# Reordering ScalarE's and GpSimd's work inside one loop of a two-layer convolution kernel

## The chip, the cores and the metric

The kernel runs on one core of one Trainium2 chip. The metric is the device time of one execution in microseconds (us), lower is better. Time before: 3071.7 us, the median of three runs (3067.76 to 3073.29).

## The reference, cut to what matters

The input x is 4 images of 64 channels and 256 x 256 points, all in fp32. Two residual layers follow each other. The change touches the first layer only:

```python
def _L0_conv_ref(x, ...):            # called with _gn(x): group norm, 32 groups
    h = _gelu(_conv2d(x, c1_w, ((1, 1), (1, 1))) + c1_b)       # 3x3, 64 -> 64
    h = _c1x1(h, c2_w, c2_b)                                   # 64 -> 128
    xa, k = jnp.split(h, 2, axis=1)
    xs = _conv2d(xa, sh_w, ((0, 0), (1, 1)), groups=C) + sh_b  # 1x3 per channel
    xs = _conv2d(xs, sv_w, ((1, 1), (0, 0)), groups=C) + sv_b  # 3x1 per channel
    xs = _gelu(xs)
    ...                              # gate from the mean of xs, keeps 2 of 3 experts
    for i, (w1, b1, w2, b2, w3, b3) in enumerate(experts):
        e = _c1x1(_c1x1(k, w2, b2) * _c1x1(xs, w1, b1), w3, b3)
        out = out + e * mask[:, i]
    return _c1x1(out, proj_w, proj_b)
x = x + _L0_conv_ref(_gn(x), ...)
x = x + _L1_conv_ref(_gn(x), ...)    # 3x3, batch norm, relu, 3x3, batch norm, relu
```

## The kernel before, in words

**Units and slots.** Layer 0 is cut into 64 units of 16 image rows (16 units to an image; 128 partitions are two row blocks of 64 channels). One loop runs over 67 slots; in slot u the 3x3 convolution of unit u is made, while unit u+1 is prepared and units u-1 and u-2 go through the taps that follow. A slot has no barrier at its end: each engine has its own list of instructions, executes it in order, and waits by semaphores for the others.

**The order is written by hand.** `at_slot(u, pos, call, ...)` files a call under slot u and a position. Positions 0 to 6 make the first half of a slot and 6 to 12 the second. All calls are sorted by slot and position, and every engine's list is exactly in that order. The position decides therefore only what stands ahead of what on one engine.

**What a slot does**, with the lines of the profile:

- The 3x3 convolution is of Winograd's kind along rows. GpSimd makes six combinations of rows of x, called `v`. TensorE multiplies them in three products: `front_conv(u, (1, 2))`, `(3, 4)` and `(0, 5)` (matmuls `ps_c<-v,us` of L492; `ps_c` has two PSUM buffers). ScalarE copies two results out (`front_copy`, `mc`, L594), VectorE combines them in four steps (`butterfly_a` to `butterfly_d`, L599 to L618), and ScalarE ends with Gelu (`front_h`, `h`, L626).
- To make `v` for unit u+1: ScalarE multiplies rows of x by 4 (`x_four`, `x4`, L526) and later others by 2 and by 4 (`x_scaled`, `e` and `x`, L540 and L542). GpSimd makes two differences with `x4` (L532), four differences of x in place (L535; both in `x_differences`), then `v` 1 to 4 (`v_inner`, L556 to L559) and `v` 0 and 5 (`v_outer`, L563 and L564).
- The taps: for each half unit TensorE makes `front_taps_a` and `front_taps_b` (`ps_a<-h,av`, L492) into the one PSUM buffer `ps_a`. Between the two stands `divide`: GpSimd writes one word (`tick`, L485) after the last matmul of taps_a, and the first matmul of taps_b waits for it. ScalarE then makes `t` (`front_taps_i`, L666), VectorE adds two shifted copies (`front_taps_h`, L672, L675, L678), after which `ps_a` is free; ScalarE's second Gelu gives `xs` (`front_xs`, L694).
- In even slots TensorE makes `ps_k`, which ScalarE copies out (L716); in odd slots it makes `ps_q`, which VectorE takes (L729). Both use the one PSUM buffer `ps_p`.
- **Statistics** of the next image's x, for its group norm: `stats_piece` (L432), on ScalarE. A piece is two instructions of 128 x 1024 points with a sum each (an Identity with a shift, then a Square in place, each followed by a read of the accumulator). Image 1's pieces fall into slots 1 to 11, some three to a slot; image 2's into slots 12 to 27 and image 3's into slots 28 to 43, two to a slot.
- **The output of layer 0** (`plan_out`: loads, `ps_o` matmuls, VectorE's `y`, L831 and L836, stores) of an earlier image runs beside the loop from slot 19 on. All DMAs are issued from SyncE's queue.

So the loop has four stages: slots 1 to 11 (three pieces a slot), 12 to 18 (two pieces), 19 to 43 (two pieces and an output), 44 to 62 (an output, no pieces). Layer 1 follows.

Of the kernel before, what the change touches and what calls it, by code (L numbers as in the profile page):

```python
# [13 lines left out]
ALU = mybir.AluOpType  # L14
# [14 lines left out]
NOCT = NG // 2  # L29
CG = 4  # L30
CPAIR = CG * GP
NCH = NG // CG
# [9 lines left out]
def conv_preact_kernel(ctx: ExitStack, tc: tile.TileContext, io, col128, colset, col64):  # L42
    nc = tc.nc
# [466 lines left out]
    def x_edges(u):  # L510

        b, k = divmod(u, NCH)
        for at_k, half, row in ((0, 0, 0), (NCH - 1, 1, 9)):
            if k == at_k and u > 0:
                rows = slice(half * C, half * C + C)
                edge = xt[u][rows, row, :]
                nc.gpsimd.tensor_scalar(edge, zeros[rows, 0:W], gn1[b][rows, 0:1], None, ALU.add)

    def x_rows(u, j):
        return xt[u][:, j : j + 5 : 4, :]  # L520
# [4 lines left out]
        inner = xt[u][:, 1:9, :].rearrange("p (g r) w -> p r g w", r=4)[:, 0:2]  # L525
        nc.scalar.activation(x4s[u], inner, AF.Copy, scale=4.0)  # L526

    def x_differences(u):

        x, x4 = xt[u], x4s[u]  # L530
        for j in (1, 2):
            nc.gpsimd.tensor_tensor(x4[:, j - 1], x_rows(u, j + 2), x4[:, j - 1], ALU.subtract)  # L532
        x_edges(u)
        for r in range(0, 8, 2):
            nc.gpsimd.tensor_tensor(x[:, r : r + 2], x[:, r + 2 : r + 4], x[:, r : r + 2], ALU.subtract)  # L535

    def x_scaled(u):

# [5 lines left out]
    def at_v(i):  # L544
        return v[:, i, :, 1 : 1 + W]

    def v_pads(b):
        edges = zeros[:, 0:4].rearrange("p (a b) -> p a b", b=2)
        nc.gpsimd.tensor_scalar(v[:, 1, :, 0 : PW : PW - 1], edges, gn1[b][:, 0:1], -6.0, ALU.add, ALU.mult)

    def v_inner(u):

        if u % NCH == 0 and u > 0:
            v_pads(u // NCH)
        p, q2, e2 = x4s.pop(u), x_rows(u, 2), e2s.pop(u)
        nc.gpsimd.tensor_tensor(at_v(1), p[:, 1], p[:, 0], ALU.add)  # L556
        nc.gpsimd.tensor_tensor(at_v(2), p[:, 1], p[:, 0], ALU.subtract)
        nc.gpsimd.tensor_tensor(at_v(3), q2, e2, ALU.add)
        nc.gpsimd.tensor_tensor(at_v(4), q2, e2, ALU.subtract)  # L559

    def v_outer(u):

# [138 lines left out]
    def front_k(b, j):  # L701

        ps = bank("p", f"ps_k_{b}_{j}").rearrange("p s a b -> p s (a b)")
        for t in range(2):
            for i in range(4):
                for s in range(2):
                    half = slice(s * C, s * C + C)
                    nc.tensor.matmul(
                        ps[32 * i : 32 * i + 32, s],
                        wk[half, s, t, :],  # L710
                        hs[NCH * b + 2 * j + i // 2][half, t, i % 2 * 2 : i % 2 * 2 + 2, :].rearrange("p a b -> p (a b)"),
                        start=(t == 0),
                        stop=(t == 1),
                    )
        k_sb[b, j] = work.tile([P, 2, GF], F32, tag="k", name=f"k_{b}_{j}", bufs=1)
        nc.scalar.activation(flat(k_sb[b, j]), ps.rearrange("p s f -> p (s f)"), AF.Identity, bias=k_bias)  # L716

# [279 lines left out]
    def at_each(places, chain):  # L997
# [8 lines left out]
    TAIL = {  # L1006
        (0, 1.15): (0, 1.15), (0, 1.55): (0, 1.55), (0, 4.7): (0, 4.7), (0, 2): (0, 2), (0, 2.2): (0, 2.2),
        (0, 4): (0, 13.2), (0, 4.15): (0, 13.3), (0, 5.2): (0, 13.4), (0, 5.3): (0, 13.5), (0, 8.6): (1, 13.9),
        (0, 7): (2, 13.2), (0, 7.2): (2, 13.25), (0, 8): (3, 13.1), (0, 9): (3, 13.2), (0, 9.1): (3, 13.3),
        (1, 1.15): (3, 13.4), (1, 1.55): (3, 13.5), (1, 4.7): (4, 13.9), (1, 2): (5, 13.2), (1, 2.2): (5, 13.25),  # L1010
        (1, 4): (6, 13.2), (1, 4.15): (6, 13.3), (1, 5.2): (6, 13.4), (1, 5.3): (6, 13.5), (1, 8.6): (7, 13.9),
        (1, 8): (8, 13.2), (1, 8.1): (8, 13.3),
# [2 lines left out]
    def at_slot(u, pos, call, *args):  # L1015

        step, order = (2 * u, pos) if pos < 6 else (2 * u + 1, pos - 6)
        if u >= UNITS:
            step, order = TAIL[u - UNITS, pos]
            step += CONV1  # L1020
        at(step, order, call, *args)

    def plan_front():
        last = UNITS - 1
        at_slot(0, 0, x_load, 2)
        at_slot(0, 1.25, next, first_end, None)
        at_slot(0, 1.36, next, first_end, None)
        for u in range(SLOTS):
            if u + 3 <= last:
                at_slot(u, 0, x_load, u + 3)  # L1030
            if u <= last:
                at_slot(u, 1, front_conv, u, (1, 2))
                at_slot(u, 1.1, front_copy, u, 0)
                at_slot(u, 1.3, front_conv, u, (3, 4))
                at_slot(u, 1.35, butterfly_a, u)
                at_slot(u, 1.4, front_copy, u, 1)
                at_slot(u, 2.1, butterfly_b, u)
                at_slot(u, 4.05, butterfly_c, u)
                at_slot(u, 6.12, butterfly_d, u)
                at_slot(u, 6.13, front_h, u, True)  # L1040
                at_slot(u, 5, front_conv, u, (0, 5))
                at_slot(u, 6.14, front_h, u, False)
            if u + 1 <= last:
                at_slot(u, 0.5, x_differences, u + 1)
                at_slot(u, 1.5, x_scaled, u + 1)
                at_slot(u, 2.3, v_inner, u + 1)
                at_slot(u, 5.5, v_outer, u + 1)
            if u + 2 <= last:
                at_slot(u, 4.3, x_four, u + 2)
            if 0 <= u - 2 <= last:  # L1050
                at_slot(u, 2, front_taps_a, u - 2, 1)
                at_slot(u, 2.2, divide)
                at_slot(u, 4, front_taps_b, u - 2, 1)
                at_slot(u, 4.15, front_taps_i, u - 2, 1)
                at_slot(u, 5.2, front_taps_h, u - 2, 1)
                at_slot(u, 5.3, front_xs, u - 2, 1)
                at_slot(u, 8.6, xs_store, u - 2, 1)
            if 0 <= u - 1 <= last:
                at_slot(u, 7, front_taps_a, u - 1, 0)
                at_slot(u, 7.2, divide)  # L1060
                at_slot(u, 9, front_taps_b, u - 1, 0)
                at_slot(u, 9.1, front_taps_i, u - 1, 0)
                at_slot(u + 1, 1.15, front_taps_h, u - 1, 0)
                at_slot(u + 1, 1.55, front_xs, u - 1, 0)
                at_slot(u + 1, 4.7, xs_store, u - 1, 0)
            j = (u - 2) // 2
            if u % 2 == 0 and 0 <= j < UNITS // 2:
                at_slot(u, 8, front_k, *divmod(j, NOCT // 4))
            if u % 2 and 0 <= j < UNITS // 2:
                at_slot(u, 8, front_q, *divmod(j, NOCT // 4))  # L1070
                at_slot(u, 8.1, front_low, *divmod(j, NOCT // 4))
        for b in range(B):
            t = NCH * (b + 1)
            if b < B - 1:
                places = (t + 1, 8.3), (t + 2, 1.25), (t + 2, 1.36), (t + 2, 1.52), (t + 2, 6.15), (t + 2, 8.3), (t + 2, 9.06)
                chain = gate(b)
                for place in places:
                    at_slot(*place, next, chain, None)
            else:
                at_each(((CONV1 + 12 + n, 12.7) for n in (1, 3, 3, 4, 8, 12, 16)), gate(b))  # L1080

        at_slot(1, 1.6, weights1_load)
        at_slot(3, 6.2, weights1_top)
        chain = weights1_scale()
        at_slot(4, 1.45, next, chain, None)
        at_slot(4, 6.2, next, chain, None)
        for i, name in enumerate(("w1", "w2")):
            chain = weights1(name)
            for n in range(3):
                at_slot(7 + 3 * i + n, 6.2, next, chain, None)  # L1090

    def plan_stats(b):

        t = NCH * (b - 1) - (4 if b > 1 else -1)
        per = 11 / NCH if b == 1 else 1
        slots = [t + per * k for k in range(NCH)]
        for k in range(NCH):
            at_slot(max(int(slots[k] - 2), 0), 1.5 if slots[k] >= 3 else 0.1, stats_load, b, k, "s", 4)
            if k == 0:
                at_slot(int(slots[0]), 0.95, stats_shift, b)  # L1100
            for i in range(2):
                s = slots[k] + i * per / 2
                first = s - int(s) < 0.5
                for part in range(2):
                    at_slot(int(s), ((1.12, 4.4) if first else (6.5, 7.15))[part], stats_piece, b, 2 * k + i, part)
        e = NCH * b - 4
        places = (e, 8.3), (e + 1, 1.25), (e + 1, 1.36), (e + 2, 1.25), (e + 2, 1.36), (e + 2, 1.52), (e + 2, 6.15), (e + 3, 1.25), (e + 3, 1.36)
        chain = stats_end(b)
        for place in places:
            at_slot(*place, next, chain, None)  # L1110
        at_slot(NCH * b - 1, 5.15, scale_weights, b)
# [280 lines left out]
    for i, (b, k) in enumerate(steps):  # L1392
# [9 lines left out]
        j = i - 3 + KEEP  # L1402
# [113 lines left out]
```

## Time and profile before

| | |
|---|---|
| median of 3 runs | 3071.7 us |
| the profiled execution | 3069.24 us |
| its span, first to last instruction | 3067.4 us |
| mean granted TensorE clock | 0.911 |
| PE busy / VectorE / ScalarE / GpSimd, share of the span | 77% / 80% / 67% / 55% |
| layer 0's loop in the span | from 63.6 us to about 1340 us |

The shares are means over stages with different limits, and are to be read stage by stage. Start to start, by the first `mc` (L594) of each unit, the slots took:

| slots | us per slot |
|---|---|
| 1 to 5 | 17.4 to 18.4 |
| 6 to 11 | 19.4 to 20.9 |
| 12 to 18 | 17.9 to 22.4, mean 19.5 |
| 19 to 43 | mostly 19.85 and 20.85 in turn; 22 to 24 where a chain of statistics stands between |
| 53 to 61 | 18.93 to 19.00 |

### The profile page before, as it was taken

How to read it: one execution, taken by the hardware profiler on the slowest of the kernel's cores; microseconds unless marked ns; L12 is line 12 of the kernel's file. 1: busy time of each engine (PE TensorE's matmuls, PEld its weight loads, DVE VectorE, ACT ScalarE, POOL GpSimd, SP SyncE). 2: the span in 40 equal slices, each digit the busy share in tenths (PEclk: the TensorE clock that was granted, in tenths of full speed). 3: DMA queues.
4: the chain of work that ended last, by engine and by line, in shares of the span. 5: the costliest groups of instructions: out<-in, count | busy, mean ns of one | idle time of the engine just before them, and what ended most of it. 6: DMA issues, size and time to landing. Idle time of an engine off the chain costs nothing.

```text
span 3067.4 us, 53128 instructions
## 1 busy us (share of the span) xinstructions
PE 2372.5 (77%) x21576; PEld 1519.2 (50%) x21576; DVE 2458.7 (80%) x2793; ACT 2054.9 (67%) x2274; POOL 1675.0 (55%) x1210
## 2 busy tenths in 40 slices
PE   1888889998999999978889999998999999200000
PEld 1444445444444545545566666776888888200000
DVE  5567677888888988867788888988998999886665
ACT  6888877777776655556566767877888888433222
POOL 5877877777677877744345545645555555000000
PEclk9999999999999999999999999998999999655555
DMA  8664579999898989838889988765777764799999
GB/s 339 205 226 188 193 254 338 344 352 327 323 348 297 307 290 315 301 146 294 320 303 343 362 316 326 261 250 195 262 265 260 271 255 142 305 426 427 426 427 405
DMA packets 135573, 915.36 MB, mean 298 GB/s; under 512 B 14944, under 2 KB 15712, under 8 KB 40608
## 3 DMA queue, kind: packets, MB, share of 16 engines
q1 hardware_dynamic: 135328, 911.97, 79.6%
q8 instruction: 169, 2.77, 0.4%
q14 instruction: 76, 0.62, 0.1%
HBM read 573.74 MB, written 338.17 MB: 297 GB/s over the span
## 4 chain that ended last, share of the span: by engine, by line
PE 27%; DMA 18%; DVE 6%; issue 2%; ACT 1%; POOL 1%; SPq 0%; DVEq 0%; ACTq 0%; POOLq 0%
PE ps_h L295 17%; PE ps_h2m L295 6%; DMA y_end<-y_d 5%; DMA h<-h_d 4%; DMA out<-h 3%; DMA y<-in_xp 3%; PE ps_hm L295 3%; DMA xs_in<-xs_d 2%; DVE h L317 1%; PE ps_o L492 1%; DVE diff L352 1%; DVE odd L361 1%; DMA yn<-y_d 1%; DVE y L831 1%; DVE h L1398 1%
## 5 line engine op out<-in xcount | busy, mean ns | idle before, releaser
L295 PE MATMUL ps_h<-diff,w_q 128*128 128x512 f32 x3072 | 754.6, 400 | 11.5 <-DVE h L317 11.5
L295 PEld LDWEIGHTS ps_h<-diff,w_q 128*128 128x128 f32 x3072 | 579.2, 190 | 183.7 <-issue 29.9
L492 PE MATMUL ps_c<-v,us 64*64 64x256 f32 x9216 | 541.2, 383 | 37.4 <-DVE ps_c L612 32.7
L342 POOL TENSOR_TENSOR d<-yn 128x1024 f32<-128x1024 f32 x128 | 355.9, 2801 | 319.1 <-DMA yn<-y_d 182.1
L492 PE MATMUL ps_a<-h,av 64*64 64x512 f32 x4080 | 400.5, 506 | 88.6 <-DVE t L675 69.2
L492 PEld LDWEIGHTS ps_c<-v,us 64*64 64x64 f32 x9216 | 362.9, 135 | 189.0 <-DVE ps_c L612 40.7
L342 POOL TENSOR_TENSOR d<-h 128x1024 f32<-128x1024 f32 x127 | 312.1, 2480 | 194.6 <-DVE diff L350 133.4
L317 DVE SCALAR_TENSOR_TENSOR h<-ps_h,scale_w,m 128x1024 f32<-128x1024 f32 x256 | 323.5, 1279 | 63.5 <-PE ps_h L295 47.3
L492 PEld LDWEIGHTS ps_a<-h,av 64*64 64x64 f32 x4080 | 160.3, 136 | 369.4 <-issue 260.6
L535 POOL TENSOR_TENSOR x<-x 128x512 f32<-128x512 f32 x256 | 328.2, 1282 | 15.5
L672 DVE SCALAR_TENSOR_TENSOR t<-ps_a,m,t 128x1020 f32<-128x1020 f32 x128 | 163.6, 1278 | 201.4 <-ACT t L666 200.7
L1397 ACT ACTIVATE v<-y_end,shift,gn 128x2048 f32<-128x2048 f32 x64 | 133.8, 2092 | 279.2 <-DMA y_end<-y_d 244.0
L381 ACT ACTIVATE junk<-h,less_h 128x2048 bf16<-128x2048 f32 (+3 forms) x133 | 256.0, 1925 | 11.1 <-DVE h L317 10.9
L1398 DVE SCALAR_TENSOR_TENSOR h<-h,ss,v 128x2048 f32<-128x2048 f32 x64 | 149.8, 2350 | 120.2 <-ACT v L1397 120.2
L831 DVE SCALAR_TENSOR_TENSOR y<-ps_o,ob,y 128x1024 f32<-128x1024 f32 x128 | 163.9, 1280 | 90.6 <-PE ps_o L492 43.1
L666 ACT ACTIVATE t<-ps_a,tap_bias,m 128x1024 f32<-128x1024 f32 x128 | 153.8, 1201 | 99.3 <-PE ps_a L492 98.8
L295 PE MATMUL ps_h2m<-odd,w_q 128*128 128x512 f32 x768 | 193.2, 400 | 8.2 <-DVE odd L361 4.4
L694 ACT ACTIVATE xs<-t 128x1024 f32<-128x1024 f32 x128 | 134.5, 1051 | 94.0 <-issue 72.7
L295 PE MATMUL ps_hm<-odd,w_q 128*128 128x512 f32 x768 | 194.2, 402 | 3.7 <-DVE t L675 3.0
L352 DVE SCALAR_TENSOR_TENSOR diff<-d,gn,diff 128x1024 fp32r<-128x1024 f32 x128 | 190.3, 1517 | 4.9 <-ACT diff L345 4.9
L345 ACT ACTIVATE diff<-d 128x1024 fp32r<-128x1024 f32 x128 | 135.1, 1055 | 83.6 <-POOL d L342 82.3
L626 ACT ACTIVATE h<-ps_c,c1b 128x1024 f32<-128x1024 f32 x128 | 135.6, 1110 | 73.3 <-DVE ps_c L618 69.7
(226 smaller groups left out, 4348.0 us busy)
## 6 DMA issues: line engine op xcount, KB each, us to landing
h_d<-h SPq DMA_DIRECT2D x114, 1024.0 KB
x<-in_xc SPq DMA_DIRECT2D x64, 1280.0 KB
h<-h_d SPq DMA_DIRECT2D x64, 1152.0 KB
yn<-y_d SPq DMA_DIRECT2D x60, 1152.0 KB
xs_in<-in_xp SPq DMA_DIRECT2D x64, 1024.0 KB
xs_d<-xs SPq DMA_DIRECT2D x128, 512.0 KB
xs_in<-xs_d SPq DMA_DIRECT2D x64, 1024.0 KB
y<-in_xp SPq DMA_DIRECT2D x64, 1024.0 KB
```

What stands on the lines that cost most here:

```text
L295: nc.tensor.matmul(ps, wq[w][:, kind, kx, :], t[:, rows, kx : kx + W], start=(j == 0), stop=(j == len(terms) - 1))
L317: nc.vector.scalar_tensor_tensor(h.rearrange("p (e k) w -> p e (k w)", e=2), ps.rearrange("p e k w -> p e (k w)"), w_scale[w], m.unsqueeze ...
L342: engine.tensor_tensor(raw.rearrange("p (g r) w -> p g r w", g=2), *pair, ALU.subtract)
L352: nc.vector.scalar_tensor_tensor(lower, raw, scale, upper.bitcast(F32), ALU.mult, ALU.subtract)
L381: nc.scalar.activation(junk[rows, 0:n], flat(h), AF.Square, bias=less[name][rows], accum_out=total)
L492: last[:] = [nc.tensor.matmul(ps[o, at_out[0] : at_out[1], :], w[i], rhs[i], **flags)]
L535: nc.gpsimd.tensor_tensor(x[:, r : r + 2], x[:, r + 2 : r + 4], x[:, r : r + 2], ALU.subtract)
L626: nc.scalar.activation(hs[u][:, :, rows, :], ps, AF.Gelu, bias=c1_bias[u // NCH])
L666: nc.scalar.activation(flat(t), flat(ps), AF.Identity, bias=tap_bias, scale=sh[:, 1:2])
L672: nc.vector.scalar_tensor_tensor(t[:, :, 1:W], ps[:, :, 0 : W - 1], sh[:, 0:1], t[:, :, 1:W], ALU.mult, ALU.add)
L831: nc.vector.scalar_tensor_tensor(y, ps.rearrange("p x s w -> p x (s w)"), out_bias[b], y, ALU.add, ALU.add)
L1398: nc.vector.scalar_tensor_tensor(h, h, ss2[:, 0:1], v, ALU.mult, ALU.add)
```

## The change

The calls are the same, and so is the number of instructions on each engine. On TensorE, VectorE and SyncE the order is the same too; on ScalarE and GpSimd it changes.

- `x_scaled(u+1)` moves from position 1.5 to 1.2: ahead of the second `mc` (1.4).
- `x_four(u+2)` moves from 4.3 to 1.58: ahead of `front_taps_i` (4.15), behind `front_xs` (1.55).
- `x_differences` is cut into three pieces and made a unit sooner: `x_fourths(u+2)` at 2.4, `x_seconds(u+2)` at 6.6 (two instructions) and at 7.3 (two). It was at 0.5 for unit u+1.
- `v_inner(u+1)`: `v` 1 to 3 move from 2.3 to 1.31, ahead of the `tick` at 2.2; `v` 4 stays at 2.3.
- `stats_piece`: in a slot's first half, from 1.12 and 4.4 to 4.35 and 4.4; in the second half, from 6.5 and 7.15 to 5.4 and 9.15. `front_taps_i` of the second half stands at 9.1.
- The copy of `ps_k` moves from 8 to 9.2 (`front_k_out`), behind `front_taps_i`.

```diff
-    def x_differences(u):
-
-        x, x4 = xt[u], x4s[u]
+    def x_fourths(u):
+
+        x4 = x4s[u]
         for j in (1, 2):
             nc.gpsimd.tensor_tensor(x4[:, j - 1], x_rows(u, j + 2), x4[:, j - 1], ALU.subtract)
-        x_edges(u)
-        for r in range(0, 8, 2):
+
+    def x_seconds(u, rows):
+
+        x = xt[u]
+        if 0 in rows:
+            x_edges(u)
+        for r in rows:
             nc.gpsimd.tensor_tensor(x[:, r : r + 2], x[:, r + 2 : r + 4], x[:, r : r + 2], ALU.subtract)
...
-    def v_inner(u):
+    def v_inner(u, part=None):
...
             if u + 1 <= last:
-                at_slot(u, 0.5, x_differences, u + 1)
-                at_slot(u, 1.5, x_scaled, u + 1)
-                at_slot(u, 2.3, v_inner, u + 1)
+                if u == 0:
+                    at_slot(u, 0.5, x_differences, 1)
+                at_slot(u, 1.2, x_scaled, u + 1)
+                at_slot(u, 1.31, v_inner, u + 1, 0)
+                at_slot(u, 2.3, v_inner, u + 1, 1)
                 at_slot(u, 5.5, v_outer, u + 1)
             if u + 2 <= last:
-                at_slot(u, 4.3, x_four, u + 2)
+                at_slot(u, 1.58, x_four, u + 2)
+                at_slot(u, 2.4, x_fourths, u + 2)
+                at_slot(u, 6.6, x_seconds, u + 2, (0, 2))
+                at_slot(u, 7.3, x_seconds, u + 2, (4, 6))
...
             if u % 2 == 0 and 0 <= j < UNITS // 2:
                 at_slot(u, 8, front_k, *divmod(j, NOCT // 4))
+                at_slot(u, 9.2, front_k_out, *divmod(j, NOCT // 4))
...
-                    at_slot(int(s), ((1.12, 4.4) if first else (6.5, 7.15))[part], stats_piece, b, 2 * k + i, part)
+                    at_slot(int(s), ((4.35, 4.4) if first else (5.4, 9.15))[part], stats_piece, b, 2 * k + i, part)
```

## The prediction

> **What bounds the kernel now.** I read the table of slices first: PE is 80 to 99% busy in the loop's part (slices 2 to 17) at nearly full clock, so I ask stage by stage what keeps it from more. The windows by stage (busy time of each engine, then clock, DMA share, GB/s) say how much is missing:
>
> ```profile
> core 0: us, PE busy (x) PEld busy (x) DVE busy (x) ACT busy (x) POOL busy (x), PEclk, DMA share, GB/s
> 80.00:192.00 112.00, 96.83 (x1445) 54.20 (x1439) 65.50 (x85) 100.55 (x149) 99.10 (x91) 0.98 0.65 227
> 192.00:294.00 102.00, 81.61 (x1120) 41.20 (x1116) 69.50 (x87) 84.12 (x124) 75.06 (x68) 0.95 0.47 177
> 294.00:430.00 136.00, 115.99 (x1640) 59.91 (x1636) 97.35 (x143) 113.71 (x158) 109.47 (x102) 0.97 0.59 214
> 430.00:955.00 525.00, 480.12 (x6628) 258.66 (x6624) 429.06 (x563) 388.05 (x548) 384.36 (x355) 0.98 0.92 333
> 955.00:1330.00 375.00, 359.41 (x5048) 185.24 (x5044) 332.28 (x431) 218.29 (x271) 292.87 (x273) 1.00 0.87 298
> ```
>
> PE is busy 80% in slots 7 to 11, 85% in 12 to 18, 91% in 19 to 43 (statistics and output) and 96% in 44 to 62 (output alone). Without statistics a slot is PE's own length, 18.95 us; with them it is 20.35 on average though ACT is busy only 74%. ACT is not full; it works in the wrong order. The timeline of slot 8 shows where (start, length, engine, line; in brackets the idle time ahead and what ended it):
>
> ```profile
> 208.61 0.66 PE L492 MATMUL ps_a<-h,av 64*64 64x256 f32 x8
> 209.09 1.15 ACT L432 ACTIVATE xs_in<-xs_in,shift 128x1024 f32<-128x1024 f32 x1
> 210.23 1.05 ACT L432 ACTIVATE xs_in<-xs_in 128x1024 f32<-128x1024 f32 x1
> 211.27 1.05 ACT L432 ACTIVATE xs_in<-xs_in 128x1024 f32<-128x1024 f32 x1
> ...
> 212.31 1.19 ACT L666 ACTIVATE t<-ps_a,tap_bias,m 128x1024 f32<-128x1024 f32 x1
> ...
> 213.53 1.28 DVE L672 SCALAR_TENSOR_TENSOR t<-ps_a,m,t 128x1020 f32<-128x1020 f32 x1 [3.50 <-ACT t L666]
> ...
> 216.28 2.38 PE L492 MATMUL ps_a<-h,av 64*64 64x512 f32 x24 [1.82 <-DVE t L675]
> ...
> 220.49 2.82 PE L492 MATMUL ps_c<-v,us 64*64 64x256 f32 x48 [0.94 <-DVE ps_c L612]
> ```
>
> taps_b ended at 209.3, but `t` (L666) began at 212.31, behind four statistics; VectorE waited 3.5 us for it; PE waited for `ps_a`, then for the butterflies behind it. The waits over the loop agree: PE ps_a <- DVE t 58.7 us in 39 waits, PE ps_c <- DVE ps_c 32.7 in 33, DVE t <- ACT t 190.3 in 90. And GpSimd has room:
>
> ```profile
> POOL tick L485 <- PE ps_a L492: 269.5, 107, 8.7
> ```
>
> That is 4 us per slot of GpSimd standing at a tick with its next work behind it.
>
> **What the Trainium skill says.** (1) "PSUM — Partial Sum Buffer", section "Engine vs sequencer instructions": ScalarE, VectorE and GpSimd queues are strict FIFO. The lines above agree: L666 was ready at 209.3 and stood until 212.3. Order is thus all the change has to work with. (2) "DMA: Bandwidth & Descriptors", section "Where 436 GB/s comes from": some 358 GB/s per core on the HBM side. Here slots 19 to 43 move 333 GB/s at a share of 0.92, or 333/0.92 = 362 at 1.0, near that figure; the page of the profile has slices of 427 late in the span, so it is no hard ceiling. I use 362.
>
> **The change, part by part.** Steps from start to start on ACT: statistics 1.15 (Identity) and 1.05 (Square), L666 1.1, mc 0.5, e 0.65, x 0.96, xs 1.14, x4 0.95, h 2.0 for two, k 1.0. DVE: taps_h 2.8, a butterfly pair 1.4. GpSimd: every op 1.25, a tick 0.1. PE: product pair 2.6, taps_a 2.3, taps_b 0.5 to 0.7, k or q 1.9.
>
> *Slots 6 to 11*, H = the end of h, near the start of the next conv. Before: 2 Identity, 2 Square (4.4), k every other slot, L666: `t` at H+5.5 (6.5 with k); taps_h, then butterflies a to c: H+12.7; taps_a(1) from H+8.4, tick, taps_b to H+11.6, L666, taps_h after c to H+15.7, d, h to H+19.2 (20.2). Measured: 19.4 to 20.9, mean 20.4, so the working is 0.7 short. After: L666 first, `t` at H+1.1, taps_h to 3.9; 2 Squares, k, mc at H+3.9 (4.9), e and x to 5.4, mc to 6.0, butterflies b and c to 8.8, conv (0,5) there; xs, x4 to 8.0, L666 9.1, taps_h 12.0, d 13.4. A piece in between ends at 11.4, xs at 13.2, two Identities at 15.45, h at **H+17.4 (18.4 with k)**. With the same shortfall 18.6. Gain 1.8 to 2.0 x 6 = **12** (8 to 16). VectorE's weight work takes back at most 1 us in two of the slots.
>
> *Slots 1 to 5*: one pair stood ahead of L666, and the same working gives 17.5 against 17.9 measured: **2** (0 to 5). *Slots 0 and 1*: e waited 1.83 us for GpSimd's differences, PE 3.85 for L612 behind two statistics: **2.5** (0 to 4).
>
> *Slots 12 to 18*: one Square ahead of mc; PE's ring taps_b, L666, taps_h, taps_a closes at 17.1, against 17.9 to 18.8 in plain slots. 1.1 x 7 = **8** (3 to 12); the statistics' own chain stays.
>
> *Slots 19 to 43*, conv at 0: L666 0.35 to 1.45, Square 2.55, k 3.6, mc to 4.2, e 4.75, x 5.7, mc 6.3; the butterflies start at 5.8 anyway (VectorE is full there) and need the second mc at 7.1. The Identity at 5.4 runs from 15.2 to 16.3, where ACT stood idle for h at 17.3. So PE could reach the 18.95 of slots 53 to 61: PE's 480.1 us at their 96% are 501, a gain of 24. But a plain slot moves 7.08 MB (6912 KB, from the DMA sizes): 7.08 MB / 362 GB/s = 19.55 us, a gain of 0.8, and some five slots with chains gain nothing: 0.8 x 25 = **20** (5 to 33).
>
> *Slots 44 to 62*: nothing. VectorE and PE both are full, and cover what ACT does.
>
> *The rest at nothing, with its cover.* GpSimd: v1, v2, v3 now stand ahead of tick 2.2; they end 6.6 after the conv's start, while taps_a ends at 7.4: PE's conv covers them (v3 waits for e, ready at 4.75). Then v4, two fourths, two of v_outer, two of seconds stand ahead of tick 7.2: 8.75 us, against 7.3 of PE without output and 9.3 with it; k or q (1.9) covers the rest, by 0.15 us only in slots 12 to 18. v_outer waits there for conv (0,5); behind it stand the seconds and the tick, for which taps_b waits. If that cover goes, PE stands up to 1 us a slot in 12 to 18, which is the low end above. x_four waits for v2 (5.35) and for its load. The k copy behind L666 holds `ps_p`: the next user is `ps_o`, 7 us on, or a chain's small matmul in three slots, where 1 us is late already now. SyncE's list is unchanged; a statistics buffer comes free up to 3 us later, but loads run two slots ahead.
>
> Sum: 2.5 + 2 + 12 + 8 + 20 = 44.5. The profiled execution took 3069.24 (span 3067.4 and 1.84 around), so 3024.7; the median of the runs was 2.5 above it: **3027 us**.
>
> **Rivals.**
> - *DMA takes the gain of slots 19 to 43.* For: 0.92 of the engines' time is taken, and single stretches of 10 us stand at 1.0. Against: stretches at 0.75 lie between, where SyncE waits for `k` or `y` from VectorE. Gain there 0 to 8: 3027 + 12 to 20 = 3039 to 3047.
> - *DMA is no limit*: slots 19 to 43 reach PE's length, 24 to 33 us: 3012 to 3023.
> - *Slower, by the load under x_four.* ACT stands at L526 until x has landed, and L666 stands behind it. The load is issued some 3 us into one slot and was needed 12.5 into the next, 29 us later; now 7 into it, 23 to 24 later, with 1.6 more before L666 is late. A transfer issued at 614.0 (y_d) was waited for until 626.2, 12 us. If landing took 25.6 it would begin to cost; from 27.5 (2 us x 25 slots) it eats all of the rest. At 28, 1.5 us a slot above 20.35 less 24.5 elsewhere: +13, 3085.
> - *It doesn't do what it says*: the built order shows each move, and equal counts of instructions; excluded.
>
> **How the numbers follow.** Likeliest case 0.6; DMA takes the gain 0.2; DMA no limit 0.13; slower 0.05; gains lost among waits I don't see, within 0.2%, 0.02. Two tenths of a per cent, 6 us, is about what a measurement of this kernel can tell from no change. The ends of the likeliest case's terms that may fall together give 3008 to 3050; with the neighbours the range is 3003 to 3054.
>
> **What would show it.** Right: in slots 6 to 11 L666 of the second half directly behind h; DVE t <- ACT t and PE ps_a <- DVE t shrinking to a third; slots of 18 to 18.7 there, 17 to 17.5 in 12 to 18, 19.2 to 19.8 in 19 to 43, 18.95 from 53; tick's wait for PE below 150 us. Wrong: ACT x4 <- DMA waits (the slower rival), PE ps_a <- POOL tick above 1 us a slot, SyncE's waits for DMAs growing with slots at 20.

## The result and the profile after

The changed kernel takes **3031.8 us**, the median of four runs (3027.39 to 3037.89), against 3071.91 (3067.76 to 3073.29) for the kernel before in the same runs. The ratio is 0.9873, 95% interval 0.985 to 0.9896: faster by 40 us. The profiled execution took 3027.39 us, with a span of 3025.4.

First the windows by stage, with the columns of before. The cuts follow the units (slots 0 to 5, 6 to 11, 12 to 18, 19 to 43, 44 to 61):

```profile
core 0: us, PE busy (x) PEld busy (x) DVE busy (x) ACT busy (x) POOL busy (x), PEclk, DMA share, GB/s
69.10:177.50 108.40, 90.55 (x1296) 51.68 (x1290) 67.48 (x86) 90.44 (x133) 93.37 (x84) 0.94 0.57 197
177.50:288.10 110.60, 98.00 (x1388) 51.14 (x1384) 84.41 (x105) 100.41 (x149) 91.93 (x85) 0.95 0.56 211
288.10:421.30 133.20, 115.14 (x1636) 59.45 (x1632) 98.42 (x142) 112.39 (x158) 109.04 (x102) 0.97 0.61 212
421.30:927.20 505.90, 476.71 (x6624) 247.66 (x6619) 434.41 (x562) 390.58 (x549) 386.63 (x354) 0.99 0.93 345
927.20:1278.30 351.10, 341.08 (x4768) 174.99 (x4764) 316.62 (x415) 205.42 (x254) 278.72 (x261) 0.99 0.87 306
```

PE is now busy 98.00/110.60 = 89% in slots 6 to 11 (80% before in 7 to 11), 86% in 12 to 18 (85%), 94% in 19 to 43 (91%) and 97% from 44 on (96%). A slot gains most where the statistics stood three to a slot, and less elsewhere.

Slot 8 again, in the timeline of the kernel after:

```profile
208.49 0.66 PE L492 MATMUL ps_a<-h,av 64*64 64x256 f32 x8
209.28 1.21 ACT L677 ACTIVATE t<-ps_a,tap_bias,m 128x1024 f32<-128x1024 f32 x1
210.39 1.05 ACT L432 ACTIVATE xs_in<-xs_in 128x1024 f32<-128x1024 f32 x1
210.52 1.28 DVE L683 SCALAR_TENSOR_TENSOR t<-ps_a,m,t 128x1020 f32<-128x1020 f32 x1 [0.77 <-ACT t L677]
...
214.16 2.33 PE L492 MATMUL ps_a<-h,av 64*64 64x512 f32 x24
...
218.10 2.82 PE L492 MATMUL ps_c<-v,us 64*64 64x256 f32 x48 [0.69 <-DVE ps_c L623]
```

taps_b ends at 209.15, `t` (L677, L666 before) starts at 209.28 instead of 3 us later, and the statistics (L432) follow it. VectorE waits 0.77 us instead of 3.50, and PE's wait for `ps_a` ahead of taps_a is gone. The last line shows what is left: the butterflies (L623), 0.69 us.

The waits of the kernel after over its loop (60 to 1300 us; those of before were read from 60 to 1340, for its loop is longer):

```profile
POOL tick L485 <- PE ps_a L492: 123.0, 64, 3.8
DVE t L683 <- ACT t L677: 94.0, 75, 9.2
PE ps_c L492 <- DVE ps_c L623: 33.1, 22, 5.3
PE ps_a L492 <- DVE t L686: 20.0, 23, 3.1
PE ps_a L492 <- POOL tick L485: 9.5, 24, 2.0
```

The first went from 269.5 to 123.0, the second from 190.3 to 94.0, the fourth from 58.7 to 20.0. The third stayed (32.7 before).

Where the 40 us came from, by the first butterfly of each unit in the profiled executions (us):

| slots | before | after | difference | predicted |
|---|---|---|---|---|
| 0 to 5 | 105.8 | 108.4 | +2.6 | -4.5 |
| 6 to 11 | 122.5 | 110.5 | **-12.0** | -12 |
| 12 to 18 | 136.7 | 133.2 | -3.5 | -8 |
| 19 to 43 | 523.2 | 506.1 | **-17.1** | -20 |
| 44 to 61 | 354.0 | 351.0 | -2.9 | 0 |
| the rest | 1755.6 | 1747.1 | -8.5 | 0 |

The rest is everything behind the first butterfly of unit 62 (the start, up to unit 0, differs by 0.6). It took 1752 to 1764 us in every other kernel below, of both kinds, so its 8.5 us are read here as the chance of two executions; no run shows more. What the loop shows is 33 us. Each figure is that of one execution: in slots 0 to 5 and 6 to 11, kernels with the same code there differ by about 2 us.

Inside slots 19 to 43 the gain isn't where it was expected. Where nothing but the steady pattern runs, the pair of slots 24 and 25 took 20.84 + 19.85 = 40.7 before and takes 17.48 + 23.07 = **40.5** after (slots 40 and 41: 40.7 and 40.2). One slot is 3.4 us shorter and the next 3.2 us longer. SyncE's timeline of the kernel after, and then VectorE's, show one load of the long slot:

```profile
527.61 0.33 SPq L803 DMA_DIRECT2D y<-in_xp  x1
```

```profile
545.96 1.28 DVE L848 SCALAR_TENSOR_TENSOR y<-ps_o,ob,y 128x1024 f32<-128x1024 f32 x1 [4.21 <-DMA y<-in_xp]
```

The load of `y` is issued at 527.61, VectorE is ready for it at 541.75 and gets it 18.35 us after the issue. So it goes in most of the long slots: 25.0 us in 8 waits behind slot 19, 1.0 in 2 before. The same load (for slot 25) in SyncE's and VectorE's timelines of before:

```profile
540.87 0.33 SPq L786 DMA_DIRECT2D y<-in_xp  x1
```

```profile
562.75 1.28 DVE L831 SCALAR_TENSOR_TENSOR y<-ps_o,ob,y 128x1024 f32<-128x1024 f32 x1
```

It was used 21.9 us after its issue, without a wait. By the trace's record of its landing it had arrived at 562.33, 0.4 us ahead: it was just in time already. Why it is issued no sooner in the kernel after stands in SyncE's waits between 420 and 720 us:

```profile
SPq L803 <- DMA y_d<-y: 77.9, 13, 8.3
SPq L747 <- DVE k L746: 47.2, 8, 11.5
```

The load waits for one of two `y` buffers to be stored, and in every second slot SyncE stands in front of the store of `k` (`low_d<-k`) while stores and loads behind it are due.

### The profile page after: what moved, and what is told of

It is laid out like the page before. It is cut to its first block, busy times and chain, and to the rows that moved or that the text cites. A ratio compares the mean times of both kernels' runs of the same rounds, so it can differ in the third digit from the quotient of the medians.

```text
span 3025.4 us, 53036 instructions
## 1 busy us (share of the span) xinstructions
PE 2364.3 (78%) x21576; PEld 1504.4 (50%) x21576; DVE 2467.0 (82%) x2793; ACT 2054.0 (68%) x2274; POOL 1677.4 (55%) x1210
## 4 chain that ended last, share of the span: by engine, by line
PE 28%; DMA 18%; DVE 5%; issue 2%; ACT 1%; SPq 1%; POOL 0%; DVEq 0%; ACTq 0%
PE ps_h L295 18%; PE ps_h2m L295 6%; DMA y_end<-y_d 5%; DMA h<-h_d 4%; DMA out<-h 4%; PE ps_hm L295 3%; DMA y<-in_xp 3%; DMA xs_in<-xs_d 2%; PE ps_o L492 2%; DVE h L317 1%; DVE diff L352 1%; DVE y L848 1%; DVE odd L361 1%; DMA y_d<-y 1%; SPq L822 0%
## 5 line engine op out<-in xcount | busy, mean ns | idle before, releaser
L295 PEld LDWEIGHTS ps_h<-diff,w_q 128*128 128x128 f32 x3072 | 577.1, 189 | 180.9 <-issue 25.8
L492 PE MATMUL ps_a<-h,av 64*64 64x512 f32 x4080 | 387.9, 493 | 38.8 <-DVE t L686 28.7
L492 PEld LDWEIGHTS ps_a<-h,av 64*64 64x64 f32 x4080 | 153.9, 134 | 307.5 <-issue 204.3
L381 ACT ACTIVATE junk<-h,less_h 128x2048 bf16<-128x2048 f32 (+3 forms) x133 | 255.9, 1924 | 11.1 <-DVE h L317 10.9
L677 ACT ACTIVATE t<-ps_a,tap_bias,m 128x1024 f32<-128x1024 f32 x128 | 154.1, 1204 | 97.8 <-PE ps_a L492 97.3
L532 POOL TENSOR_TENSOR x<-x,x 128x512 f32<-128x512 f32 x128 | 161.0, 1279 | 43.3 <-ACT x L526 43.3
```

Of the source, the lines that this page charges most:

```text
L295: nc.tensor.matmul(ps, wq[w][:, kind, kx, :], t[:, rows, kx : kx + W], start=(j == 0), stop=(j == len(terms) - 1))
L381: nc.scalar.activation(junk[rows, 0:n], flat(h), AF.Square, bias=less[name][rows], accum_out=total)
L492: last[:] = [nc.tensor.matmul(ps[o, at_out[0] : at_out[1], :], w[i], rhs[i], **flags)]
L677: nc.scalar.activation(flat(t), flat(ps), AF.Identity, bias=tap_bias, scale=sh[:, 1:2])
```

## The experiments

Medians in us; the kernel before was 3070.9, 3069.8, 3071.8 and 3070.5 alongside.

**1. Either half of the change alone.** `stats_k_alone` is the kernel before with the places of the statistics and of the copy of `ps_k` alone; `stats_back` is the kernel after with the statistics at their old places.

```diff
 # stats_k_alone, to the kernel before
+                at_slot(u, 9.2, front_k_out, *divmod(j, NOCT // 4))
...
-                    at_slot(int(s), ((1.12, 4.4) if first else (6.5, 7.15))[part], ...)
+                    at_slot(int(s), ((4.35, 4.4) if first else (5.4, 9.15))[part], ...)
 # stats_back, to the kernel after
-                    at_slot(int(s), ((4.35, 4.4) if first else (5.4, 9.15))[part], ...)
+                    at_slot(int(s), ((1.12, 4.4) if first else (6.5, 7.15))[part], ...)
```

> The kernel before with the new places of the statistics and of the copy of ps_k alone; x_scaled, x_four and GpSimd's order as they were. Theory A (the gain is L666 no longer standing behind statistics): nearly all of the gain, 3027 to 3042 us, slots 6 to 11 near 18.5, PE ps_a <- DVE t below 25 us over the loop. Theory B (the multiples of x and GpSimd's earlier differences carry it): at most half, 3050 us or more.

> The changed kernel with the statistics at their old places (1.12, 4.4, 6.5, 7.15); all else as changed. Theory A: L666 stands behind two or four statistics again, and e and x now delay the second mc as well: 3062 to 3080 us, slots 6 to 11 at 20 or more. Theory B: most of the gain stays, 3030 to 3045 us.

Measured: `stats_k_alone` 3046.4 (ratio 0.991, 0.9889 to 0.9931), `stats_back` 3069.0 (0.9986, 0.9971 to 1.0001). The parts give 25 and 2 us, the two together 40. The second is what theory A said; the first lies between what the two theories gave (up to 3042, from 3050). By stage, against before:

| slots | stats_k_alone | stats_back | both |
|---|---|---|---|
| 0 to 5 | +7.9 | +7.3 | +2.6 |
| 6 to 11 | -12.3 | -3.9 | -12.0 |
| 12 to 18 | -0.4 | +0.1 | -3.5 |
| 19 to 43 | -17.3 | -1.4 | -17.1 |
| 44 to 61 | +0.2 | -4.5 | -2.9 |

The statistics' places earn the gain of slots 6 to 11 and of 19 to 43 by themselves. So theory A holds there, and there is more to the total: the earlier work on x earns slots 44 to 61 by itself and, in company with the other part, slots 12 to 18. Most of what the two give beyond their sum stands in slots 0 to 5, where either alone costs 7 to 8 us and both together 2.6; no run shows why. The waits over the loop of `stats_back`, where VectorE again waits 149.6 us for `t`, suggest that freeing GpSimd without freeing ScalarE mostly moves the wait to the butterflies (32.7 us before):

```profile
POOL tick L485 <- PE ps_a L492: 96.4, 58, 3.8
PE ps_c L492 <- DVE ps_c L623: 52.4, 42, 5.5
```

And those of `stats_k_alone`, where GpSimd still stands 248.1 us at its ticks, show that it already runs into `y`'s load:

```profile
DVE y L837 <- DMA y<-in_xp: 26.2, 9, 5.1
```

**2. GpSimd's pieces.** `seconds_ahead` is the kernel after with both pairs of `x_seconds` ahead of the tick at 7.2.

```diff
-                at_slot(u, 6.6, x_seconds, u + 2, (0, 2))
-                at_slot(u, 7.3, x_seconds, u + 2, (4, 6))
+                at_slot(u, 6.6, x_seconds, u + 2, (0, 2, 4, 6))
```

> The changed kernel with all four of GpSimd's differences of x at 6.6, ahead of the tick at 7.2, instead of two ahead and two behind. By the prediction's count 11.3 us of GpSimd then lie between the two ticks, against 9.2 of TensorE's work (k or q among it) in slots without an output and 11.2 with one: taps_b waits some 2 us a slot in slots 1 to 18 and 0 to 0.3 later, 3055 to 3070 us. If GpSimd's order hardly matters: within 4 us of 3031.8.

Measured: 3118.7 (1.0151, 1.0131 to 1.0172), 87 us slower than the kernel after. Slots 0 to 18 took 402.3 instead of 352.1 us, 19 to 43 516 instead of 506, 44 to 61 378.3 instead of 351.1. Its waits between 65 and 1300 us:

```profile
PE ps_a L492 <- POOL tick L485: 111.3, 74, 4.6
```

PE waits 1.5 us for the tick, 74 times. Between two ticks GpSimd has nine operations of 1.25 us, 11.3, where PE has 9.2, or 11.2 with an output, k or q among it. With seven (8.75) the wait is 9.5 us over the whole loop. So GpSimd's work between two ticks is worth counting, as the prediction did, but the count isn't exact: it put this kernel at 3055 to 3070. In slots with an output it gave a wait of 0 to 0.3 us, and PE waits 36.9 us in slots 19 to 43 and 29.3 in 44 to 61, some 1.5 a slot. No run shows what the count leaves out.

**3. What limits slots 19 to 43.** Three explanations of the wait for `y`'s load: (a) SyncE stands in front of `low_d<-k` and issues late; (b) two `y` buffers are too few; (c) the transfers issued in a burst ahead of it take too long. Each was tried alone.

```diff
 # low_later_before, low_later_after: the store of k behind those of y and xs
-        nc.sync.dma_start(low_d[b][:, j, :], low)
+        low_out[b, j] = low
...
+    def low_store(b, j):
+        nc.sync.dma_start(low_d[b][:, j, :], low_out.pop((b, j)))
...
+                at_slot(u, 8.65, low_store, *divmod(j, NOCT // 4))
 # third_y_after: a third buffer for y (a small tile gives its room)
-        spread = lstat.tile([P, P], F32, tag="spread", ...)
+        spread = lstat.tile([P, 1, W], F32, tag="h_end", ...)[:, 0, 0:P]
-        ys[b, k] = chunk_out(f"y_{b}_{k}", "o", 2)
+        if k % 3 == 2 and 2 * k < (NOCT, NOCT, 22, 0)[b]:
+            ys[b, k] = front_pool.tile([P, CPAIR, W], F32, tag="y3", name=f"y_{b}_{k}")
+        else:
+            ys[b, k] = chunk_out(f"y_{b}_{k}", "o", 2)
 # half_loads_before, half_loads_after: a statistics load in two left out
+        if b >= 2 and k % 2:
+            x_in[b, k] = x_in[b, k - 1]
...
-        nc.sync.dma_start(flat(x_in[b, k]), io["xp"][b, k])
+        if b < 2 or k % 2 == 0:
+            nc.sync.dma_start(flat(x_in[b, k]), io["xp"][b, k])
```

> The same move of low's store in the kernel before. Both theories: no compute waits for a DMA there (VectorE's y for y's load 1.0 us in all), so within 3 us of 3071.9. If it gained 6 us or more, SyncE's order would have cost time before the change as well.

> The changed kernel with the store of low (which waits for VectorE's k, L746, in odd slots) behind the stores of y and xs in SyncE's queue. Theory C (in slots 19 to 43 the 16 DMA engines' rate is the limit, 7.08 MB a slot): even slots stay at 20.8 to 21.2, the time within 4 us of the changed kernel, 3027 to 3036. Theory D (SyncE's queue is the limit: y's store stands 4.5 us behind low's, so y's next load lands late): the store of y goes out 4 us sooner in odd slots, VectorE's y no longer waits for y's load in even slots, those take 19.3 to 19.8, and the time is 3016 to 3024 us.

> The changed kernel with a third buffer for y (every third chunk of the output stage in the loop), so that y's next load need not wait for the store of the chunk before last. Bytes and rates are the same. Theory C (the DMA engines' rate): slots 23 to 31 stay near 164 us for the eight, the time within 4 us of 3031.8. Theory E (two buffers and a landing time of 18 us: load, add, store and load again don't fit into two slots, and the DMA engines idle 12 to 14% of each even slot meanwhile): no wait of VectorE's y for its load, the eight slots 152 to 158 us, 3010 to 3022 us in all.

> The kernel before with the same loads left out. If ScalarE's order is the limit there: nothing changes, slots 23 to 31 at 164 to 165 us for the eight, 3065 to 3073 us. If DMA was the limit before the change as well: 155 to 160 for the eight.

> The changed kernel with every second load of the statistics of images 2 and 3 left out (the pieces run on the chunk before instead, so those statistics are not the reference's): 0.52 MB less of 7.08 MB a slot in slots 12 to 43, all instructions of the five engines as before. Theories C and E both: less in the queues, VectorE's y waits little for its load, slots 23 to 31 take 152 to 156 us for the eight, 3008 to 3020 us. If the limit were something else than DMA: 164 us for the eight, 3027 to 3036.

| kernel | median | ratio (95%) | slots 19 to 43 | DVE y <- DMA y, 420 to 1300 us |
|---|---|---|---|---|
| low_later_before | 3068.9 | 0.9995 (0.9986 to 1.0004) | 523.1 | none |
| half_loads_before | 3070.2 | 0.9997 (0.9987 to 1.0008) | 521.7 | none |
| low_later_after | 3032.0 | 0.9865 (0.9844 to 0.9886) | 504.9 | 27.0 in 8 |
| third_y_after | 3034.9 | 0.9883 (0.9861 to 0.9906) | 506.4 | 25.8 in 8 |
| half_loads_after | 3032.2 | 0.987 (0.9844 to 0.9896) | 501.6 | 21.9 in 8 |

Each alone does next to nothing to the time, in either kernel (`half_loads_after` takes 4.5 us off the stage, and misses the 3008 to 3020 that both theories gave it). The kernel before doesn't wait for transfers there: VectorE stood 1.0 us in all for `y`'s load. `half_loads_before` says little beside that, since the same loads left out do little in the kernel after either. For the kernel after two readings were left: that none of the three is the cause, or that one takes the other's place. SyncE's waits between 420 and 720 us spoke for the second. First `low_later_after`, then `third_y_after`:

```profile
SPq L808 <- DMA y_d<-y: 71.2, 13, 9.0
```

```profile
SPq L747 <- DVE k L746: 70.6, 8, 11.5
```

With `low_d` later SyncE stood less in front of it (22.9 us for 47.2), and the load still waited for its buffer (71.2). With a third buffer that wait is gone, and SyncE stood in front of `low_d<-k` instead (70.6 for 47.2). Issuing sooner didn't land sooner: measured from the short slot's second `y` (568.89 after, 565.48 and 567.86 in these two), the load was issued 0.9 us ahead in the kernel after, 2.5 in `low_later_after` and 4.2 in `third_y_after`, and VectorE began with it 17.2, 17.1 and 17.4 us behind. What stands ahead of it in the queue was left. In `half_loads_after`, the load that was left out was not the one ahead of `y`'s in the queue. SyncE's timeline in its odd slot reads:

```profile
552.14 0.32 SPq L750 DMA_DIRECT2D low_d<-k  x1
...
558.68 0.34 SPq L412 DMA_DIRECT2D xs_in<-in_xp  x1
562.26 0.33 SPq L806 DMA_DIRECT2D y<-in_xp  x1
```

Where the fence has its mark stand the stores of `y` and `xs` and the loads of `x`, `ranks` (two) and `xs_in`: from 552.14 to 558.68 eight transfers are issued, and `y`'s load is the next. The statistics load (L412) that stayed is in that burst; the one left out would have stood between 535 and 546, where SyncE issues nothing else.

**4. The causes together.** Three kernels, built on the kernel after:

```diff
 # other_half_loads: the other half left out, those inside the burst
+        if b >= 2 and k % 2 == 0 and k > 0:
+            x_in[b, k] = x_in[b, k - 1]
...
 # third_y_low_later: third_y_after and low_later_after together
 # third_y_first: third_y_low_later, and y's load ahead of all others of its slot
-                at_slot(u - 1, 2.0, out_load, b, k)
+                at_slot(u - 1, -0.1, out_load, b, k)
```

> The changed kernel with the other half of the statistics' loads of images 2 and 3 left out (even chunks but the first; those statistics are not the reference's). The loads left out before were those outside the burst in which y's late load stands; these stand in it, directly ahead of y's load: 1.05 MB less of some 7 MB in the burst. Theory C (the burst's bytes): y lands 3 us sooner, VectorE's y waits 0 to 1.5 us instead of 4, slots 23 to 31 take 153 to 158 us for the eight, 3018 to 3026 us. If the landing of y has nothing to do with the bytes ahead of it: 162 to 165.

> The changed kernel with both: a third buffer for y and low's store behind the stores of y and xs. Alone, each only moved the place where SyncE stands (y's load behind y's store, or low's store behind VectorE's k), and the DMA engines still idled 12 to 17% of every even slot. If SyncE standing is the limit in slots 19 to 43 (theory D+E): the idle time goes, slots 23 to 31 take 154 to 158 us for the eight, 3018 to 3025 us in all. If it is the rate in the burst between an odd and an even slot (theory C): 162 to 165 for the eight, within 4 us of 3031.8.

> The changed kernel with three buffers for y, low's store behind, and y's load issued first in a slot (ahead of the loads of x, ranks, xs and the statistics) instead of last. Same bytes. Theory F (y is late only because it stands last in the burst): VectorE's y waits for no load, slots 23 to 31 take 152 to 156 us for the eight, 3012 to 3022 us. Theory C: another load, xs_in or x, becomes the late one; 160 to 165 for the eight, within 5 us of 3031.8.

| kernel | median | ratio (95%) | slots 19 to 43 | a steady pair (24, 25) | DVE y <- DMA y |
|---|---|---|---|---|---|
| after | 3031.8 | 0.9873 (0.985 to 0.9896) | 506.1 | 17.48 + 23.07 | 25.0 in 8 |
| third_y_low_later | 3025.3 | 0.9837 (0.9809 to 0.9865) | 493.0 | 17.47 + 21.51 | 11.1 in 6 |
| third_y_first | 3022.9 | 0.984 (0.9813 to 0.9867) | 493.3 | 17.48 + 23.99 | 0.4 in 1 |
| other_half_loads | 3012.4 | 0.9804 (0.978 to 0.9828) | 486.6 | 17.47 + 19.66 | 3.9 in 2 |

`other_half_loads` is the one that frees the stage. It leaves out about as many bytes as `half_loads_after`, which did next to nothing, but from the burst ahead of `y`'s load: 19 us, more than expected, and the long slot falls from 23.07 to 19.66. (Both kernels run those statistics on other data than the reference's; they are made for their times alone.) One burst kept its load, for the first chunk of an image is not left out, and there the wait came back. SyncE's and VectorE's timelines of `other_half_loads`:

```profile
554.25 0.34 SPq L412 DMA_DIRECT2D xs_in<-in_xp  x1
557.95 0.33 SPq L806 DMA_DIRECT2D y<-in_xp  x1
```

```profile
576.94 1.28 DVE L851 SCALAR_TENSOR_TENSOR y<-ps_o,ob,y 128x1024 f32<-128x1024 f32 x1 [3.52 <-DMA y<-in_xp]
```

So (c) is what makes the load late: what stands ahead of it in the queue. (a) and (b) matter together only. `third_y_low_later` takes 13 us off the stage, although `y`'s load still stands behind the same transfers. With the load first, VectorE's wait is gone (0.4 us), yet two slots of 24 to 25 us stay (25 and 43). The delay then falls on another load of the burst, as PE's timeline of `third_y_first` shows in slot 25:

```profile
537.57 1.88 PE L492 MATMUL ps_o<-xs_in,m 64*64 64x512 f32 x8 [2.15 <-DMA xs_in<-xs_d]
```

`third_y_first` and `third_y_low_later` leave nothing out and lie 7 to 9 us under the kernel after, but their intervals overlap with its own: the stage (493 against 506 us) shows the gain, the total alone does not. The eight slots from 23 on took 159.0 and 157.7 us, between the figures of the theories.

What holds the burst up can be read from the trace's records of landings, which the views don't show. A transfer reports its landing in parts, nearly always 16. Of `y`'s load of 527.61 in the kernel after, twelve parts had landed by 536.27; the last four came between 544.60 and 545.88, and VectorE began at 545.96. So it is with most transfers of slots 19 to 43: in 174 of 183 the largest gap is the one behind the twelfth part, and the last part comes 7.8 us (median) behind the twelfth. The load that PE waits for in slot 25 of `third_y_first` had twelve parts by 522.87 and the last at 537.44. The store of 529.65, for whose end the next load of `y` waits, had twelve by 539.83 and the last at 549.57.

The records also name a suspect. The loads of `ranks` (256 KB, two in every second slot) report four parts with their data instead of 16. From 110 us to the first of them, at 397.87, no last part came more than 2.2 us behind the twelfth. Over one pair of them (517.89 and 519.13) the lag grows from 5.1 us, for the load of `x` ahead, to 11.4, for the load of `xs_in` behind. So what is late is a quarter of each transfer, and it seems to queue behind `ranks`. No kernel here loads `ranks` in another way: this is read from the records and not shown by an experiment.

**5. Slots 0 and 1.** `third_y_seconds` is `third_y_first` with both pairs of `x_seconds` behind the tick in slots 0 and 1.

```diff
-                at_slot(u, 6.6, x_seconds, u + 2, (0, 2))
+                at_slot(u, 7.25 if u < 2 else 6.6, x_seconds, u + 2, (0, 2))
```

> The version with the third y buffer, low's store later and y's load first, and in slots 0 and 1 alone both pairs of x_seconds behind the tick of the second half (7.25 and 7.3) instead of one pair ahead of it. Theory: in slot 1 of the changed kernel PE waited 2.04 us for the tick, because GpSimd made two fourths, two of v_outer and two seconds ahead of it (before, the same wait was 0.96); with 2.6 us of seconds behind the tick it ends by PE's own time, the wait goes below 0.7 and slots 0 to 5 take 105 us instead of 107. Rival: the wait is replaced, because the seconds then push v 1 of the next unit past the next conv's start or taps_a's end; slots 0 to 5 stay at 107 or grow. In total the kernel stays at 3019 to 3024; a difference of 2 us can be told in the stage only.

Measured: 3023.5 (0.9849, 0.9819 to 0.9879); slots 0 to 5 took 107.1 us, 107.0 in `third_y_first`. PE's timeline of slot 1 in the kernel after, and then in `third_y_seconds`:

```profile
91.19 4.39 PE L492 MATMUL ps_c<-v,us 64*64 64x256 f32 x48 [5.26 <-DVE ps_c L623]
99.77 0.44 PE L492 MATMUL ps_a<-h,av 64*64 64x256 f32 x3 [2.04 <-POOL tick L485]
```

```profile
99.30 0.44 PE L492 MATMUL ps_a<-h,av 64*64 64x256 f32 x3 [0.24 <-POOL tick L485]
...
108.54 0.66 PE L492 MATMUL ps_a<-h,av 64*64 64x256 f32 x8 [1.26 <-POOL tick L485]
```

The wait for the tick went from 2.04 in the kernel after (1.62 in `third_y_first`) to 0.24, as the theory said; against `third_y_first` slot 1 fell by 1.4 us and slot 2 grew by 1.7, because the tick of slot 2 (at 108.54) now stands behind the seconds. The rival was right: the wait was replaced. The wait for the butterflies stays above the 3.85 us of before: 5.26 in the kernel after, 5.42 in `third_y_seconds`. ScalarE's timeline in the kernel after says why:

```profile
85.93 0.63 ACT L549 ACTIVATE e<-x 128x512 f32<-128x512 f32 x1 [1.94 <-POOL x L540]
...
87.56 0.58 ACT L605 ACTIVATE mc<-ps_c 128x512 f32<-128x512 f32 x1
```

In slot 1 `e` still waits for GpSimd's differences, and with `x_scaled` moved to 1.2 the second `mc` (L605), which the butterflies wait for, stands behind it: 87.56, against 85.87 before. TensorE's products for slot 1 had ended at 85.92, so `e` holds `mc` up by some 1.6 us at most. No kernel undid this alone, so its part in the slot is argued, not shown.

## Why the prediction was right, point by point

- **The total** was 3027, measured 3031.8, and the likeliest case held. Against the profiled execution's own time the sum said 3024.7, measured 3027.39. But the 33 us that the loop shows are less than the 44.5 of the sum, and about 8 us of the agreement come from the rest of the program, where nothing was predicted: that is luck. The sum also counts 0.8 us in all 25 slots of 19 to 43 although it says that some five gain nothing; by its own words that term is 16, and the sum 40.5.
- **The signs named ahead** came in part. The tick's wait fell to 123.0 (below 150), PE's for `ps_a` to a third (20.0), VectorE's for `t` only to half (94.0). Slots 6 to 11 took 17.3 to 19.1 us, near the 18 to 18.7. But 17 to 17.5 was reached in two of slots 12 to 18 alone, and the steady slots from 19 on took 17.48 and 23.07 in turn where 19.2 to 19.8 was named.
- **Slots 6 to 11, 12 us: right**, in size and cause. -12.0 measured, 18.4 us a slot where 18.6 was worked out, and `stats_k_alone` reaches it with the statistics' places alone. The Trainium skill's strict FIFO ("PSUM — Partial Sum Buffer", "Engine vs sequencer instructions") carried it: `t` starts 0.13 us behind taps_b where it stood 3 us.
- **Slots 0 to 5, 4.5 us: wrong, there is no gain.** The step counted only what ScalarE gained. In slot 1 the second `mc` is held by `e`, which waits for GpSimd, and the tick by fourths, v_outer and seconds. Measured +2.6. The other kernels with the changed code there took 106.4 to 107.6, and two with the code of before 105.8 and 106.5, so that the loss lies between nothing and 2.6 us. That either half of the change alone costs 7 to 8 us here wasn't foreseen.
- **Slots 12 to 18, 8 us: the right direction, half the size.** 3.5 measured. The step took PE's ring of 17.1 us for all seven slots; slots 12 and 16 reach it (17.24, 17.17), but slot 13 has 19.37, and the chain slots 14 and 18 still take 21.6 and 20.9.
- **Slots 19 to 43, 20 us: the size right, the term wrong.** 17.1 measured. The prediction spread it as 0.8 us over each plain slot, from bytes at 362 GB/s. Measured: next to nothing in slots 23 to 30 (-0.3 in the eight) while one load is late; nearly all of it in slots 19 to 22 (-7.9) and slots 31 to 43, among which chains stand (-9.0). That these add up to the forecast is luck. Nor was the limit a mean rate. Between 500 and 600 us the kernels before and after moved 350 GB/s alike, and `third_y_low_later` 362, with the same bytes a unit. Of the figures in the Trainium skill's "DMA: Bandwidth & Descriptors", "Where 436 GB/s comes from", some 358 is thus near what this stretch holds on average, though slices of it reach 444. But the average did not set the slot: `half_loads_after` moved 330 there and gained 4.5 us in the stage, `other_half_loads` 349 and gained 19.5.
- **The rival "DMA takes the gain of slots 19 to 43"** named the right resource and the wrong form. It expected 0 to 8 us there because the engines are full; the kernel before, at a share of 0.98 between 500 and 600 us, waited 1.0 us in all for `y`'s load. What takes the gain is how late the last parts of one transfer come.
- **The rival "DMA is no limit"** is what `other_half_loads` comes to: 486.6 us in the stage, 36.6 under before, more than the 24 to 33 it was given. That kernel leaves loads out; no kernel with all of them got there.
- **The slower rival, `x_four` behind its load:** no wait of `x4` for a DMA over the loop. The late load was `y`'s, not x's.
- **Slots 44 to 61, nothing: 2.9 us too little.** The 18.95 us taken for PE's own length was not its floor: slots 53 to 61 now take 167.6/9 = 18.62. `stats_back` gains 4.5 here and `stats_k_alone` nothing, so it is the work on x. VectorE and PE did not cover all of it.
- **GpSimd's cover** held for the change: 9.5 us of waits for ticks. The count behind it fell short at two operations more: 111.3 us of waits, and 3118.7 where it gave 3055 to 3070.

## What to carry to other kernels

Where an engine is idle for a quarter and others still wait for it, write down its list around one slot and ask what stands ahead of the instruction that the bounding engine needs; a move that costs nothing can give 2 us a slot. Two such moves on two engines can be worth more together than apart (here 40 us against 25 and 2), so undo each before calling it useless. Ahead of predicting a gain, look for the transfer that arrives just in time already: its slack, and not the mean share of the DMA engines, says how much of the gain it will let through. And look at when its parts land: a transfer is as late as the last of them.

## What the runs showed of the hardware that was not expected

- A share of busy DMA engines near 1 didn't tell a limit. Between 500 and 600 us the kernel before had 0.98 at 351 GB/s, and VectorE stood 1.0 us in all for `y`'s load from slot 19 on; the kernel after had 0.93 at 350, and VectorE stood 25.0.
- Inside these 100 us the rate swings. The DMA view of the kernel after, in slices of 2.5 us (busy share in tenths, 9 for 90% or more, then the rate):

```profile
DMA  9993999999999999998289899999999999936999
GB/s 406 424 388 147 262 329 375 387 317 422 415 418 285 301 415 428 414 428 352 125 221 295 367 434 302 409 419 433 294 270 416 403 444 419 408 153 198 294 369 418
```

  Rates of 415 to 444 alternate with slices at 125 to 153, one in every two slots, each at the end of a stretch in which SyncE issues nothing (541 to 549 us for one). The share in them is 2 to 3 tenths, and 4 of 16 are 2.5.
- A transfer's parts need not land together. Of `y`'s load of 527.61, 1 MB, twelve of 16 parts had landed 8.7 us after the issue, and the last four 16.99 to 18.27 us after it. Alone, at the 420 GB/s of the best slices, 1 MB would take an estimated 2.5 us. This began with the first load whose landing comes in four parts (`ranks`, at 397.87).
